# Cross-attention block on one core: first keys by token halves, residuals by quarters, sums of fc_w on GpSimd

## The chip, the cores and the metric

The kernel runs on 1 core of one Trainium2 chip. The metric is the device time of one execution in microseconds (us), the median over several runs. Engines are named as the profile names them: PE (TensorE, with its weight loads PEld), DVE (VectorE), ACT (ScalarE), POOL (GpSimd), SP (the engine from whose queue nearly all DMAs are issued).

## What is computed

One transformer block with cross-attention, in float32, for 8 batches of 256 tokens with 512 features, 16 heads of 32, and an MLP of 2048:

```python
def block(hidden_states, encoder_hidden_states, mask):
    x = layer_norm(hidden_states, ln1_w, ln1_b)
    q, k, v = x @ q_w + q_b, enc @ k_w + k_b, enc @ v_w + v_b      # 16 heads of 32
    attn = softmax(where(mask, q k^T / sqrt(32), -max))
    hidden = (attn v) @ cproj_w + cproj_b + hidden_states
    y = layer_norm(hidden, ln2_w, ln2_b)
    return hidden + gelu(y @ fc_w + fc_b) @ proj_w + proj_b
```

## The kernel before

**Tiling.** The batches are taken in 4 groups of 2 (512 tokens). All dense products are 2 by 2 block products by Strassen's scheme in 7 products: each operand has four quarters "11", "12", "21", "22" and three more slices for sums ("s2", "s3", "s4" of a weight, `A_SUMS`; "t1", "t2", "t4" of the tokens, `B_SUMS`), made by `sum_up` on an engine given by name. `strassen` returns seven closures p0 to p6, one for each product; a product of the projections is 4 matmuls of 256 columns in the code. The one exception is `eight`, which makes the first group's keys (`pkT`) as four plain quarter products k[0] to k[3], since these need no sums.

**Attention.** A group has 8 units (4 head groups by 2 batches). The loop over `units` issues for unit n, in this order: scores of unit n+2, softmax of n+2 (DVE L555, ACT L565), transposes of the probabilities of n (`turn_probs`, `ppt` L590, copied by DVE L593 and ACT L595), `divide` of n+1 on POOL (L579, four operations), and `attend` (`av`, L606). In between stand the lists `between[g, u, 0/1]`, which hold products of the next group's projections and transpositions (`turn_ctx` `pct`, `turn_x` `pxt`, `turn_hid` `pyt`), and `aside[g, u, 0..3]`, which hold loads, sums and the steps of the layer norms (`norm_over`: statistics, roots, `normalise` at L197). `begin` and `spread` put work there. Projected q, k and v go to DRAM and come back by head group (`load_qk`, `load_v`). `later` holds stores that are issued after `attend`.

**Output projection and residual.** `project_out(g)` gives `po`: products p0 to p6, u1 at L357 on DVE with the bias `cb`, the others at L362, L371 and L512; POOL L513 adds each quarter to the residual tile `resx`, one load of 1 MB for the group (`load_res`), whose quarter "12" first gets `cbd`, a difference of the bias halves (`bias_res`, POOL L506). Two stores write the sum to `hid_dram`. Group 3's projection follows the last unit, with the attention's last sums (`sum_att`, L626) on DVE.

**MLP.** It starts when the last projection is through, and runs group by group: four q, each with 7 products of fc (`pf`, L877; sums u and h on DVE at L932 to L949, gelu on ACT L920, sums of h on POOL L952 and L953), then 7 products of proj (`py`). In the first group, fc_w's quarters q+1 are summed on DVE (`sum_fc`, L167) while q runs; fcw[0] is summed on POOL in group 3's last units. fcw_3 takes the place of `cw` and is loaded after the attention; then follow on SP the four quarters `pw` of proj_w (1 MB each), `resm` (the hidden state for the residual, 1 MB, read back from `hid_dram`), and `hm` for the next group. POOL adds `projb` to all of `resm` at once (L959); DVE sums `pw` in four operations (L886).

**What sets the order.** The order is written out by hand: the program is recorded under a manual schedule, so each engine runs its instructions in the order of the code, and each DMA is issued from SP in the order of the code. A DMA has one of 8 semaphores and is issued when the eighth DMA before it is through. The 8 loads of the rows of biases and layer norm weights (`rows`) are issued from POOL; `turn_cols` turns them to columns (`cols`), which `made` of the keys needs.

The prologue ahead of the unit loop is, in its first part:

```python
        run(turn_ctx(0))
        load_ctx(1)
        ws["c"] = weight("cw", cproj_w)
        k, q, v, tx = project_qk(0, "kT"), project_qk(0, "qT"), project_v(0), turn_x(0)
        seen, roots, normalise = layer_norm(xs[0], "a0")
        run([k[0], *seen, roots, k[1], *normalise])
```

## Time and profile before

| What | Value |
|---|---|
| median of 3 runs | 761.43 us (761.0 to 761.65) |
| the profiled execution's own time | 761.83 us |
| its span in the profile | 759.6 us |
| granted PE clock, mean | 0.998 |
| busy: PE, DVE, ACT, POOL | 742.5, 367.9, 295.6, 379.1 us |
| data moved by DMA | 68.69 MB, 90 GB/s on the mean |
| MLP's first product starts, by the chain of waits | 361.79 us |
| one q of fc (7 products), one group of proj | 12.09 us, 48.36 us |

The span runs from the first to the last recorded instruction; the execution's own time is 2.2 us longer. A timeline line gives start, duration, engine, line of the code, operation, output and inputs, and in brackets the idle time ahead of it with the instruction that ended it. The waits list sums these idle times by the line that waited and the one waited for. A matmul of float32 is recorded as two instructions, so a Strassen product of the projections, 4 matmuls in the code, shows as x8.

### The profile page before, as it was taken

What the parts mean: (1) busy time and instruction counts of PE and PEld (TensorE: products, weight loads), DVE (VectorE), ACT (ScalarE), POOL (GpSimd) and SP (SyncE); (2) the same over time, 40 slices, a digit from 0 to 9 for tenths busy, and PEclk for the clock granted to TensorE, in tenths of its full rate; (3) what the DMA queues carried; (4) which work ended last, traced back from release to release, by engine and by line L of the source; (5) the groups of instructions that cost most, each with busy time, mean ns of one, the idle gap of its engine ahead of it and who ended that gap; (6) DMA issues with size and microseconds to landing.
All of it is one profiled execution on the core that took longest, in us unless ns stands there. A gap on an engine that the chain in (4) does not pass through costs nothing.

```text
span 759.6 us, 12080 instructions
## 1 busy us (share of the span) xinstructions
PE 742.5 (98%) x4441; PEld 624.1 (82%) x4441; DVE 367.9 (48%) x968; ACT 295.6 (39%) x857; POOL 379.1 (50%) x330
## 2 busy tenths in 40 slices
PE   7999999999999999898999999999999999999997
PEld 6988877887788777677888888888888888888886
DVE  3666755666466566657478442234412255122011
ACT  2267677766676777751332001230003300032200
POOL 3747599648664578996444520525305145032340
PEclk9999999999999999999999999999999999999999
DMA  9624522462234357423760004000040000200001
GB/s 297 220 70 129 168 85 81 130 211 70 98 106 150 98 182 246 145 70 111 228 215 2 1 0 167 1 0 1 1 144 22 2 1 0 77 36 0 1 1 56
DMA packets 55914, 68.69 MB, mean 90 GB/s; under 512 B 4740, under 2 KB 37552, under 8 KB 55728
## 3 DMA queue, kind: packets, MB, share of 16 engines
q1 hardware_dynamic: 55600, 67.91, 27.1%
q8 instruction: 35, 0.57, 0.3%
q14 instruction: 23, 0.19, 0.1%
q0 software_dynamic: 256, 0.02, 0.0%
HBM read 46.95 MB, written 20.97 MB: 89 GB/s over the span
## 4 chain that ended last, share of the span: by engine, by line
PE 91%; DVE 2%; ACT 2%; POOL 2%; DMA 1%; issue 1%; SPq 0%; DVEq 0%; POOLq 0%
PE pf L877 25%; PE py L877 25%; PE pqT L338 6%; PE ppt L590 6%; PE pv L338 5%; PE po L338 5%; PE av L606 5%; PE s L537 5%; PE pkT L338 4%; PE pkT L436 2%; ACT pr L565 1%; POOL x L197 1%; PE pct L210 1%; PE pyt L210 1%; PE pxt L210 1%
## 5 line engine op out<-in xcount | busy, mean ns | idle before, releaser
L877 PE MATMUL pf<-y,fcw 128*128 128x256 f32 x896 | 194.3, 379 | 0.8 <-DVE u L934 0.8
L877 PEld LDWEIGHTS pf<-y,fcw 128*128 128x128 f32 x896 | 170.2, 190 | 24.2 <-DVE u L934 1.2
L579 POOL TENSOR_TENSOR pr<-pr,rsum 128x512 f32<-128x512 f32 x128 | 129.4, 1042 | 74.9 <-DVE rsum L577 43.6
L565 ACT ACTIVATE pr<-pr,nmax 128x256 f32<-128x256 f32 x256 | 128.2, 503 | 60.5 <-DVE nmax L555 60.4
L555 DVE CUSTOM_DVE_ANT_0 pr<-s,mb 128x256 f32<-128x256 f32 x256 | 94.1, 413 | 46.2 <-PE s L537 33.2
L952 POOL TENSOR_TENSOR hs<-h,h 128x512 f32<-128x512 f32 x16 | 22.8, 1426 | 174.0 <-PE pf L877 127.5
L877 PE MATMUL py<-pw,h 128*128 128x256 f32 x384 | 84.9, 379 | 0.0
L877 PE MATMUL py<-pw_t,h 128*128 128x256 f32 x384 | 83.5, 379 | 0.0
L877 PEld LDWEIGHTS py<-pw_t,h 128*128 128x128 f32 x384 | 72.8, 190 | 9.7
L877 PEld LDWEIGHTS py<-pw,h 128*128 128x128 f32 x384 | 72.7, 190 | 9.7
L590 PEld LDWEIGHTS ppt<-ident,pr 128*128 128x128 f32 x512 | 57.3, 141 | 14.6 <-issue 9.0
L590 PE MATMUL ppt<-ident,pr 128*128 128x128 f32 x512 | 68.6, 276 | 0.2
L930 ACT COPY u<-pf 128x512 f32<-128x512 f32 x16 | 9.3, 584 | 150.0 <-PE pf L877 148.9
L920 ACT ACTIVATE h<-h,cols 128x256 f32<-128x256 f32 x96 | 43.4, 501 | 28.7 <-DVE h L949 14.2
L595 ACT COPY pt<-ppt 128x512 f32<-128x512 f32 x96 | 51.6, 571 | 4.9 <-PE ppt L590 4.9
L338 PE MATMUL pv<-vw,ctxT 128*128 128x256 f32 x224 | 52.4, 380 | 0.0
L920 ACT ACTIVATE h<-pf,cols 128x256 f32<-128x256 f32 x32 | 13.4, 470 | 98.1 <-PE pf L877 98.1
L338 PE MATMUL pqT<-xnT,qw 128*128 128x256 f32 x224 | 51.0, 379 | 0.0
L565 ACT ACTIVATION_READ_ACCUMULATOR pr<-pr,nmax 128x1 f32 x256 | 48.6, 190 | 0.0
L338 PEld LDWEIGHTS pv<-vw,ctxT 128*128 128x128 f32 x224 | 41.0, 190 | 5.4 <-ACT xnT L312 0.3
L338 PEld LDWEIGHTS pqT<-xnT,qw 128*128 128x128 f32 x224 | 41.3, 190 | 4.9
L606 PE MATMUL av<-pt,v 128*32 128x256 f32 x512 | 38.6, 386 | 2.9 <-ACT pt L595 2.1
(126 smaller groups left out, 970.0 us busy)
## 6 DMA issues: line engine op xcount, KB each, us to landing
ctx<-in_ctx_dram SPq DMA_DIRECT2D x16, 256.0 KB, 4.6
x<-in_x_dram SPq DMA_DIRECT2D x16, 256.0 KB, 5.4
v_dram<-st_v SPq DMA_DIRECT2D x16, 256.0 KB, 2.1
v<-v_dram SPq DMA_DIRECT2D x16, 256.0 KB, 3.9
resx<-in_x_dram SPq DMA_DIRECT2D x4, 1024.0 KB, 6.4
hid_dram<-resx SPq DMA_DIRECT2D x8, 512.0 KB, 2.8
hm<-hid_dram SPq DMA_DIRECT2D x16, 256.0 KB, 5.9
fcw<-in_L_xattn_fc_w_dram SPq DMA_DIRECT2D x16, 256.0 KB, 6.0
```

The lines of the kernel that those rows point to most:

```text
L210: nc.tensor.transpose(ps[:, ts(t, P)], xt[:, ts(c, P)], ident)
L338: nc.tensor.matmul(bank[n][:, i, :], l[:, c, ts(i, P)], r[:, c, :], start=first and i == 0 and c == 0, stop=last and c == HC - 1, skip_gro ...
L537: nc.tensor.matmul(banks[j][:, i, :], qT[j * HD : (j + 1) * HD, b * S + i * P : b * S + (i + 1) * P], kT[j * HD : (j + 1) * HD, b * SK : ( ...
L555: nc.vector.tensor_tensor_reduce(pr[:, j, i, :], banks[j][:, i, :], mbias[g][1][:, b, :], scale=-SCALE, scalar=FLT_MAX, op0=ALU.add, op1=A ...
L565: nc.scalar.activation(pr[:, j, i, :], pr[:, j, i, :], AF.Exp, bias=nmax[:, j, i : i + 1], scale=-1.0, accum_out=sums[:, j, i : i + 1],)
L579: nc.gpsimd.tensor_tensor(pr[:, j], pr[:, j], rsum[:, j, :, None].to_broadcast([P, NQ, SK]), ALU.mult,)
L590: nc.tensor.transpose(ps[:, kc, ts(i, P)], probs[n][:, j, i, ts(kc, P)], ident)
L595: nc.scalar.copy(pt, ps)
L606: nc.tensor.matmul(av[j * HD : (j + 1) * HD, :], vs[g, hg][:, b * NK + kc, ts(j, HD)], pts[n, j][:, kc, :], start=(kc == 0), stop=(kc == N ...
L877: nc.tensor.matmul(ps, lhsT, rhs, start=first, stop=last, skip_group_check=True)
L920: nc.scalar.activation(h[n][q][:, i, :], src[:, i, :], AF.Gelu_apprx_tanh, bias=col(c_fcb, half * HF + 2 * q + i), scale=1.0,)
L952: nc.gpsimd.tensor_tensor(h["s3"][q], h["11"][q], h["21"][q], ALU.subtract)
```

## The change

- **Start.** The first loads come in the order ctx_0, ctx_1, k_w's quarters 11 and 12, ctx_2, ctx_3, k_w's 21 and 22. Twelve transpositions of the constant `ident` into a PSUM tile that nobody reads are issued first. The first group's context is turned by token halves (`turn_first_ctx`), k[0] and k[1] stand behind one half each, and the sums of that context, formerly taken from PSUM on DVE, are made on POOL. pkT's last quarter is done in matmuls of 256 columns instead of 128.
- **Layer norms.** `norm_over` takes an engine; the statistics stand earlier and the normalise steps one or two to a slot. The one for `hm` goes from POOL to DVE.
- **Residuals.** `resx` becomes four tiles of a quarter each, loaded, biased, added and stored by the quarter. Group 0's are loaded at the end of unit 0 of group 1.
- **Group 3.** The slots of the 14 products and of the four `pyt` change; the sums of fcw[0] come earlier.
- **MLP.** The sums of fcw[1] to fcw[3] go from DVE to POOL; those of proj_w become 16 pieces on DVE; POOL adds the bias to two quarters of `resm` instead of all, and DVE adds it at u1 of `py` instead of ACT's copy. A_SUMS has another order of the same sums.

```diff
         a = Operand(wts.tile([P, 7, HC, S], F32, tag="w", bufs=4, name=name))
+        load_quarters(a, w, f, QUARTERS)
+        return a
+    def load_quarters(a, w, f, which):
...
             at = f + at * step
-            nc.sync.dma_start(a[n], src[:, k : k + HC, at : at + S])
-        return a
+            if n in which:
+                nc.sync.dma_start(a[n], src[:, k : k + HC, at : at + S])
...
         ("s3", "11", "21", ALU.subtract),
-        ("21", "21", "22", ALU.add),
-        ("s2", "21", "11", ALU.subtract),
+        ("s2", "22", "s3", ALU.subtract),
+        ("21", "s2", "11", ALU.add),
...
-    def load_tiles(pool, src, tag, name):
+    def load_tiles(pool, src, tag, name, between=None):
...
         for t in range(NT):
+            if between and t == NT // 2:
+                between()
...
                     nc.scalar.copy(chunk(x, c), halves(ps))
-                    sums = (second, x["t2"], x["t1"]), (first, x["t4"], x["t2"])
-                    if g:
-                        sums += ((second, x["12"], x["12"]),)
+                    sums = (
+                        (second, x["t2"], x["t1"]),
+                        (first, x["t4"], x["t2"]),
+                        (second, x["12"], x["12"]),
+                    )
...
             return [lambda c=c: piece(c) for c in (0, 2, 1, 3)]
+        def turn_first_ctx():
+            def piece(k):
+                if k == 0:
+                    ctxT[0] = tokens_operand(both, "cT", "ctxT_0")
+                for j in range(2):
+                    ps = turned(f"pct_0_{k}_{j}").rearrange("p (c s) -> p c s", c=HC)
+                    for t in range(2):
+                        for c in range(HC):
+                            nc.tensor.transpose(
+                                ps[:, c, ts(t, P)], ctxs[0][2 * k + t][:, ts(HC * j + c, P)], ident
+                            )
+                    to = ctxT[0][QUARTERS[2 * j + k]]
+                    if j == 0:
+                        nc.vector.tensor_copy(to, ps)
+                    else:
+                        nc.scalar.copy(to, ps)
+            return [lambda k=k: piece(k) for k in range(2)]
...
             if g == 0 and tag == "kT":
-                return [lambda n=n: eight(f"p{tag}_{g}", n, ws[w], src(), made) for n in QUARTERS]
+                return [lambda n=n: eight(f"p{tag}_{g}", n, ws[w], src, made) for n in QUARTERS]
...
             turns[0] ^= 1
-            step = P if n == "22" else S
...
                 for c in range(NC):
-                    for t in range(0, S, step):
-                        nc.tensor.matmul(
-                            bank[:, i, t : t + step],
-                            w[f"{n[0]}{c // HC + 1}"][:, c % HC, ts(i, P)],
-                            x[f"{c // HC + 1}{n[1]}"][:, c % HC, t : t + step],
-                            start=i == 0 and c == 0 and t == 0,
-                            stop=c == NC - 1,
-                            skip_group_check=True,
-                        )
+                    nc.tensor.matmul(
+                        bank[:, i, :],
+                        w[f"{n[0]}{c // HC + 1}"][:, c % HC, ts(i, P)],
+                        x()[f"{c // HC + 1}{n[1]}"][:, c % HC, :],
+                        start=i == 0 and c == 0,
+                        stop=c == NC - 1,
+                        skip_group_check=True,
+                    )
...
-        def load_res(g):
-            res[g] = residual(work, group_of(xf, g), "res", f"resx_{g}")
...
-        def quarter_of_res(g, n):
+        def quarter_of(src, n):
             o, k = int(n[0]) - 1, int(n[1]) - 1
-            return res[g][:, 2 * k : 2 * k + 2, ts(o, S)]
-        def bias_res(g):
-            r = quarter_of_res(g, "12")
-            nc.gpsimd.tensor_tensor(r, r, by_tiles(cbd), ALU.add)
+            return src[k * S : (k + 1) * S, ts(o, S)].rearrange("(t p) d -> p t d", p=P)
+        def load_res(g, *which):
+            for n in which:
+                r = work.tile([P, 2, S], F32, tag=f"res{n}", bufs=1, name=f"resx_{g}_{n}")
+                nc.sync.dma_start(r, quarter_of(group_of(xf, g), n))
+                res[g, n] = r
+                if n == "12":
+                    nc.gpsimd.tensor_tensor(r, r, by_tiles(cbd), ALU.add)
...
             def made(n, bank, u):
-                r = quarter_of_res(g, n)
+                r = res[g, n]
...
                 nc.gpsimd.tensor_tensor(r, r, st, ALU.add)
-                if n == "12":
-                    later.append(lambda: store_hid(g))
-            def store_hid(g):
-                for k in range(2):
-                    nc.sync.dma_start(
-                        hid_dram[g][k * S : (k + 1) * S, :].rearrange("(i p) d -> p i d", p=P),
-                        res[g][:, 2 * k : 2 * k + 2, :],
-                    )
+                later.append(lambda: nc.sync.dma_start(quarter_of(hid_dram[g], n), r))
...
-        def start_norm(g, tiles, tag):
-            norms[tag] = layer_norm(tiles[g], f"{tag}{g}", GP)
+        def start_norm(g, tiles, tag, eng):
+            norms[tag] = layer_norm(tiles[g], f"{tag}{g}", eng)
...
-        def norm_over(g, tiles, of_, tag, places):
-            begin(g, *places[0], start_norm, of_, tiles, tag)
+        def norm_over(g, tiles, of_, tag, places, eng=nc.gpsimd):
+            begin(g, *places[0], start_norm, of_, tiles, tag, eng)
...
                 norm_over(
-                    g, xs, g + 2, "a", [(2, 1), (2, 2), (3, 1), (3, 2), (3, 3), (4, 1), (4, 1), (4, 2), (4, 2)]
+                    g, xs, g + 2, "a", [(2, 1), (2, 1), (2, 2), (2, 2), (2, 2), (3, 1), (3, 2), (4, 1), (4, 2)]
...
         g = 1
-        begin(g, 1, 3, load_res, 0)
-        begin(g, 2, 2, bias_res, 0)
+        begin(g, 0, 3, load_res, 0, *QUARTERS)
...
         sums_at(att_in, 1, [(g, 6, 1), (g, 6, 2), (g, 7, 1), (g, 7, 2)])
-        begin(g, 5, 3, load_res, 1)
-        begin(g, 6, 2, bias_res, 1)
+        begin(g, 5, 3, load_res, 1, "11", "22", "21")
+        begin(g, 6, 3, load_res, 1, "12")
...
             project_out(1) + project_out(2),
-            [(u, i, 1) for u in range(8) for i in range(2) if (u, i) not in ((3, 1), (7, 1))],
+            [(u, i, 1) for u in range(8) for i in range(2) if (u, i) not in ((6, 1), (7, 1))],
         )
-        begin(g, 3, 3, load_res, 2)
-        begin(g, 4, 2, bias_res, 2)
-        begin(g, 7, 3, load_res, 3)
-        begin(g, 7, 3, bias_res, 3)
+        for u, h, which in (
+            (2, 2, ("11",)), (3, 2, ("22", "21")), (4, 2, ("12",)), (5, 3, ("11",)), (7, 3, ("22", "21"))
+        ):
+            begin(g, u, 3, load_res, h, *which)
...
         norm_over(
-            g, hids, 0, "m", [(1, 1), (1, 2), (2, 1), (2, 2), (2, 3), (3, 1), (3, 2), (4, 1), (4, 2)]
+            g, hids, 0, "m", [(1, 1), (1, 2), (2, 1), (2, 2), (2, 2), (3, 1), (3, 2), (4, 1), (4, 2)], V
...
-        for c, (u, i) in enumerate(((5, 1), (6, 1), (7, 1), (7, 1))):
+        for c, (u, i) in enumerate(((6, 1), (6, 1), (7, 1), (7, 1))):
...
             fcw[q] = weight(f"fcw_{q}", fc_w, q * S)
-        def sum_fc(q, *which):
-            sum_up(V, fcw[q], A_SUMS, *which)
...
             g,
-            [(5, 2), (6, 2), (6, 3), (7, 2)],
+            [(2, 2), (2, 3), (4, 2), (5, 2)],
...
-        load_ctx(0)
-        ws["k"] = weight("kw", k_w)
+        warm = ps_t.tile([P, G], F32, tag="pt", name="warm")
+        for t in range(12):
+            nc.tensor.transpose(warm[:, ts(t % NT, P)], ident, ident)
+        ws["k"] = Operand(wts.tile([P, 7, HC, S], F32, tag="w", bufs=4, name="kw"))
+        ctxs[0] = load_tiles(
+            work, group_of(ef, 0), "ctx", "ctx_0", lambda: load_quarters(ws["k"], k_w, 0, ("11", "12"))
+        )
+        load_quarters(ws["k"], k_w, 0, ("21", "22"))
...
-        run(turn_ctx(0))
+        first = turn_first_ctx()
+        k, q, v, tx = project_qk(0, "kT"), project_qk(0, "qT"), project_v(0), turn_x(0)
+        seen, roots, normalise = layer_norm(xs[0], "a0")
+        run([first[0], k[0], first[1], k[1]])
...
         ws["c"] = weight("cw", cproj_w)
-        k, q, v, tx = project_qk(0, "kT"), project_qk(0, "qT"), project_v(0), turn_x(0)
-        seen, roots, normalise = layer_norm(xs[0], "a0")
-        run([k[0], *seen, roots, k[1], *normalise])
+        run([*seen, roots, k[2], *normalise])
...
         make_mask(0)
-        run([k[2], *tx])
+        run([*tx, k[3]])
...
         sum_up(V, xnT[0], B_SUMS, 0, 1)
-        run(k[3:])
...
         sum_up(GP, ws["v"], A_SUMS, *ALL)
-        nc.gpsimd.tensor_tensor(cbd, cb[:, :S], cb[:, S:], ALU.subtract)
+        sum_up(GP, ctxT[0], B_SUMS, 0, 1)
         run(q[:1])
-        sum_up(GP, ctxT[0], B_SUMS, 2)
...
         run([roots, q[5]])
+        sum_up(GP, ctxT[0], B_SUMS, 2, 3)
+        nc.gpsimd.tensor_tensor(cbd, cb[:, :S], cb[:, S:], ALU.subtract)
...
         o = project_out(3)
+        load_res(3, "12")
...
             )
-        def sum_pw(i):
-            to, a, b = (("t1", "12", "11"), ("t2", "22", "t1"), ("12", "22", "12"), ("t4", "21", "t2"))[i]
-            nc.vector.tensor_tensor(pw[to], pw[a], pw[b], ALU.subtract)
+        def sum_pw():
+            for to, a, b, op in (
+                ("12", "22", "12", ALU.subtract),
+                ("t2", "12", "11", ALU.add),
+                ("t1", "22", "t2", ALU.subtract),
+                ("t4", "21", "t2", ALU.subtract),
+            ):
+                for p in range(0, HF, 2):
+                    c = slice(p, p + 2)
+                    nc.vector.tensor_tensor(pw[to][:, c], pw[a][:, c], pw[b][:, c], op)
+                    yield
+        pw_sums = sum_pw()
+        pbd = wpool.tile([P, HD2], F32, name="pbd")
+        nc.gpsimd.tensor_tensor(pbd, projb[:, :HD2], projb[:, HD2:], ALU.subtract)
...
+            def out_quarter(b, k):
+                return ht[:, 2 * b : 2 * b + 2, ts(k, HD2)]
+            def by_tiles(row):
+                return row[:, None, :].to_broadcast([P, 2, HD2])
...
                 ahead = g == 0 and q + 1 < HF // 2
+                def some_pw(n):
+                    if g == 0 and q:
+                        for _ in range(n):
+                            next(pw_sums)
...
                 if ahead:
-                    sum_fc(q + 1, 0, 1)
+                    sum_up(nc.gpsimd, fcw[q + 1], A_SUMS, 0, 1)
+                some_pw(1)
...
                 if ahead:
-                    sum_fc(q + 1, 2, 3)
+                    sum_up(nc.gpsimd, fcw[q + 1], A_SUMS, 2, 3)
+                some_pw(2)
...
                 nc.vector.tensor_tensor(h["21"][q], bank[5], u2, ALU.add)
+                some_pw(1)
...
                 nc.gpsimd.tensor_tensor(h["21"][q], h["21"][q], h["22"][q], ALU.add)
-                if g == 0:
-                    for i in ((), (0,), (1, 2), (3,))[q]:
-                        sum_pw(i)
...
                     ht = residual(work, hid_dram[g], "resm", f"resm_{g}")
-                    nc.gpsimd.tensor_tensor(
-                        ht, ht, projb[:, None, :].to_broadcast([P, NT, D]), ALU.add
-                    )
+                    for b, bias in ((0, projb[:, :HD2]), (1, pbd)):
+                        o = out_quarter(b, 0)
+                        nc.gpsimd.tensor_tensor(o, o, by_tiles(bias), ALU.add)
...
             }
-            def out_quarter(b, k):
-                return ht[:, 2 * b : 2 * b + 2, ts(k, HD2)]
...
             proj(bank[1], "11", "11", True, False)
-            nc.scalar.copy(u1, bank[1])
+            nc.vector.tensor_tensor(u1, bank[1], by_tiles(projb[:, HD2:]), ALU.add)
+            if g == 0:
+                for _ in pw_sums:
+                    pass
```

## The prediction

> **What bounds the kernel now.** I read the busy line and the shares of the chain first, then the waits of TensorE (PE), then timelines around each place that the diff touches.
>
> ```profile
> PE 742.5 (98%) x4441; PEld 624.1 (82%) x4441; DVE 367.9 (48%) x968; ACT 295.6 (39%) x857; POOL 379.1 (50%) x330
> ...
> PE 91%; DVE 2%; ACT 2%; POOL 2%; DMA 1%; issue 1%; SPq 0%; DVEq 0%; POOLq 0%
> ```
>
> PE holds 91% of the chain. The number of products stays the same, so the change can win only PE's waits, and lose by new ones. They are few (us in total, times, longest):
>
> ```profile
> PE pct L210 <- DMA ctx<-in_ctx_dram: 5.1, 4, 3.5
> PE av L606 <- ACT pt L595: 2.1, 2, 1.9
> PE po L338 <- DVE po_u L357: 1.8, 1, 1.8
> PE pxt L210 <- POOL x L197: 1.6, 2, 1.1
> PE pf L877 <- DVE u L934: 0.8, 1, 0.8
> ```
>
> Next the timeline at these places (start, duration, engine, line):
>
> ```profile
> 6.48 3.03 PE L210 MATMUL pct<-ident,ctx 128*128 128x128 f32 x13 [0.17 <-DMA ctx<-in_ctx_dram]
> 100.11 8.40 POOL L197 TENSOR_SCALAR x<-x,mv_a,rstd_a 128x512 f32<-128x512 f32 x4
> 108.56 0.77 PE L210 MATMUL pxt<-ident,x 128*128 128x128 f32 x5 [1.12 <-POOL x L197]
> 316.87 1.53 PE L606 MATMUL av<-pt,v 128*32 128x256 f32 x16 [1.91 <-ACT pt L595]
> 349.33 1.49 DVE L626 TENSOR_TENSOR att<-att 128x256 f32<-128x256 f32 x1
> 352.88 3.73 PE L338 MATMUL po<-cw,att 128*128 128x256 f32 x16 [1.82 <-DVE po_u L357]
> 375.82 1.27 POOL L952 TENSOR_TENSOR hs<-h,h 128x512 f32<-128x512 f32 x1 [9.45 <-ACT h L920]
> 377.75 4.29 SPq L226 DMA_DIRECT2D resm<-hid_dram  x1
> 390.78 4.53 POOL L959 TENSOR_TENSOR resm<-resm,projb 128x2048 f32<-128x2048 f32 x1 [12.34 <-DMA resm<-hid_dram]
> 393.52 4.02 DVE L167 TENSOR_TENSOR fcw<-fcw 128x512 f32<-128x512 f32 x2
> 407.48 3.72 PE L877 MATMUL pf<-y,fcw 128*128 128x256 f32 x16 [0.79 <-DVE u L934]
> ```
>
> The reader should see that POOL waits idle for `resm` until 390.78 and nobody minds, because the `fcw` sums run on DVE. Below, T0 = 361.79 is where the MLP's first product starts; from there PE is packed but for the 0.79.
>
> [...] the 13 transposes above take 0.233 each, the later ones 0.109. No later PE wait exceeds 1.91[...]. [...] L952 at 395.28 starts as the waiting L959 ends. [...] two fcw sums on DVE take 4.02 beside L959's 4.53, but 1.41 at 381.43; an L626 sum takes 1.43 to 1.49 on DVE beside POOL's fcw sums.
>
> **Part by part** (PE time, negative is faster).
>
> 1. *First keys by halves.* Half of ctx and k's quarters 11, 12 are loaded first. The four ctx tiles now land at about 3.4, 4.2, 5.7, 6.4, so k's two quarters take the third and fourth place and the last is here by 6.5 to 7[...]. Eight transposes and a copy (.4 to .6) put k[0] at about 6.2 to 6.5 and, at 16 × .216 = 3.46, its end near 9.8. But `turn_cols` stands behind k[0], and `rows` is whole only at 11.05 (last issue on POOL's queue 5.35, 5.7 to landing). PE waits about 1.3, then turns the other half (8 × .109) and waits for its copy: k[1] at 12.85 instead of 13.36. To q: 2 × 3.455 + 1.75 + 3.455 = 12.12, against 12.42 before (pkT_22 in half-width matmuls costs .12 more, the rest is small gaps). q starts at 24.97 for 25.78: **−0.8** (0 to −2). Moving four ctxT sums to POOL and cbd behind them is covered by PE's seven q products (12.1).
> 2. *Statistics earlier, one normalise per slot.* Four L197 in a row (8.40) hold PE at 108.56 and 187.91. Start to start the stalled transposes take 2.21 and 1.58, unstalled .87: 1.34 + .71 = **−2.05** (−1.5 to −2.1). At the places of the new order POOL has slots between its divides (4 × 1.01 of a period near 8 to 11).
> 3. *Residuals by quarters, group 1.* The four loads of group 0's residual are now issued at the end of unit 0 and the bias add on quarter 12 is put at once on POOL, ahead of the next divide (L579, at 142.43 before). On SP they stand behind x (issued 139.94), mask and v_1, which is issued at 142.84 and lands 5.1 later, at 147.94. Two 256 KB quarters more make 149.5 for quarter 12; add 1.27, then divides at 1.01: pr0 at 151.8, pr1 at 152.9. PE's ppt of that unit started at 150.74 and needs them: **+1.65** (0.5 to 2.8). Behind that add wait only the four divides, for which ppt waits. The same pattern in the other groups has its load issued where the queue is short: 0. The 12 more loads and 8 more stores put about 20 × .45 = 9 us on SP, over 280 us and among loads made a unit or more ahead: 0 (up to +0.5). Stores now wait on L513 in SP's FIFO, with the next kT, qT and v loads behind them, a unit ahead of need: 0.
> 4. *Group 3.* A product now fills slot (3,1), where the 1.91 wait stood: the period stays at 8.08. Its place (6,1) is freed of 1.73, and one transposition (4 × .13) goes from (5,1) to (6,1), where unit 5's 8.33 falls to 8.08: −1.73 − .25 + .45 = −1.5, near −1.6 with the shorter `av`. The fcw[0] sums leave the last slots for (2,2) to (5,2); then DVE's three L626 (1.43 + 1.49 + 1.48) run at about .45 each and po_u is ready before PE asks. From the end of the last `av`'s pieces to T0 it is 15.29, where 1.0 + 7 × 1.727 = 13.1 is needed: −2.2. Against it the hm normalise comes to DVE (4 × .48, in softmax slots) and two loads wait on POOL: +.5. **−3.3** (−2 to −4.2).
> 5. *MLP.* The fcw sums move from DVE to POOL, the projection sums become 16 pieces of .69 on DVE, the residual's bias add becomes 2 × 1.27 on POOL and another row on DVE. The 0.79 at 407.48 came from L886's 2.28 + 3.35 ahead of u: **−0.8**. But POOL's order becomes hs and h of q=0, both `resm` adds (they wait for the load), then fcw[2]'s sums. [...] PE's second product of q=2 needs s3 and s2 at T0 + 24.17 + 1.73 = T0 + 25.9 (two q of 12.09). Before, resm landed at T0 + 28.9; no one noticed. In the changed kernel the last hid store is one quarter, so fcw_3 is issued from about T0 + 2.65 (before T0 + 5.02), its last quarter lands between T0 + 7.4 and T0 + 10.0 (before T0 + 12.4), and the chain of pw and resm loads adds 16.5: T0 + 23.9 to 26.5, I take 25.1. Then 2 × 1.27 (adds), 2 × 1.27 (s3, s2), .15 to be seen: T0 + 30.3. **+4.4** (2.4 to 6.0; nothing excludes less if the queue drains sooner, hence rival A). Behind POOL's wait are s4, `21` and hs of q=1; PE needs the first two in the same q, later, the rest at T0 + 48.
>
> Sum: −0.8 − 2.05 + 1.65 − 3.3 − 0.8 + 4.4 = −0.9. The profiled execution took 761.83 (span 759.6 and 2.2 around it): 760.9. It stands 0.4 above the median of 761.43, so 760.5.
>
> **Rivals.** *A, the resm wait is hidden.* If resm lands before T0 + 20.7 (25.9 less 5.2 of POOL work), the +4.4 falls away: 756.1. For: SP's queue is ahead of before and quarters are smaller. Against: 1 MB of fcw_3, 4 MB of pw and 1 MB of resm are moved in order, and they took 24 from the first issue before. *B, slower: the clock drops.* [...] a matmul that takes .216 takes .43[...]: 760.5 + 2.6 = 763.1, and 764.7 if the wait is 6.0. [...] PE may keep its clock. *C, the group-1 divide is on time* (quarter 12 landed before 148.4, as the v_1 load is not what limits it): −1.65, 758.9. *D, the start doesn't do what it says*, since rows bind k[0]'s end rather than the context: 0 instead of −0.8, 761.3.
>
> **How the numbers follow.** About 0.2% (1.5 us) is what a measurement of this kernel can tell from no change. Forecast with D: .45, between 759 and 762.5; C .12; A .18; B .25. A and most of C are faster, B is mostly slower, and the forecast's middle lies 0.9 below before, so a third of it passes the lower bound: faster .40, same .36, slower .24. The likeliest is 760.5. Leaving out a tenth at either end, in A's lower and B's upper half, gives 756.0 to 764.3.
>
> **What would show it.** In the changed profile: PE waits for POOL L167 `fcw` once near T0 + 26 for about 4.4, with `resm` adds before it; no `pxt` waits; a ppt wait on POOL L579 near 150 of about 1.65; no po_u wait; pkT_11 near 6.4 and a wait at ps_cols; the granted clock at 9 in the slice of the fcw wait, or lower if B is right. A resm landing before T0 + 20.7, or a PE wait of several us at another place, would make it wrong.

## The result and the profile after

The changed kernel took 767.63 us on the median of 6 runs (764.47 to 769.32), the kernel before 762.53 on the same chip. The ratio is 1.0066, with a 95% interval of 1.0039 to 1.0092: slower by 0.4 to 0.9%. The prediction said 760.5, 0.9 less than before, with a range of 756.0 to 764.3. The profiled execution took 769.02 (span 767.2), 7.2 more than the profiled one of before.

I read the profile in the same order as before. The busy line and the shares of the chain:

```profile
PE 749.7 (98%) x4437; PEld 628.9 (82%) x4437; DVE 360.5 (47%) x970; ACT 293.0 (38%) x851; POOL 378.3 (49%) x346
...
PE 84%; POOL 6%; issue 3%; DMA 2%; ACT 2%; DVE 1%; SPq 1%; POOLq 0%; DVEq 0%
```

PE is busy for 7.2 us more. The twelve transpositions of the constant account for 2.8 of that; the products are otherwise nearly the same, so some of them ran slower. And POOL's share of the chain has grown from 2% to 6%. The waits of PE (us in total, times, longest):

```profile
PE pf L903 <- POOL fcw L171: 5.7, 1, 5.7
PE ppt L610 <- POOL pr L599: 3.3, 5, 2.0
PE warm L796 <- POOL neg_half L110: 1.4, 1, 1.4
PE ps_cols L476 <- DMA rows<-in_L_xattn_fc_b_dram: 1.1, 1, 1.1
PE av L626 <- ACT pt L615: 0.4, 2, 0.2
PE pkT L462 <- DVE ctxT L324: 0.3, 1, 0.3
```

The waits on L210, po_u and u are gone as forecast, the forecast waits on fcw and pr are there, both longer than forecast. To find where time was won and lost I set the starts of `av` (one for each unit) beside each other, from the timelines of both kernels:

| Landmark | before | after | shift |
|---|---|---|---|
| group 0, unit 0 | 63.69 | 62.84 | -0.85 |
| group 0, unit 5 | 110.99 | 108.95 | -2.04 |
| group 0, unit 6 | 119.29 | 118.41 | -0.88 |
| group 1, unit 1 | 148.53 | 147.66 | -0.87 |
| group 1, unit 2 | 159.55 | 162.97 | +3.42 |
| group 1, unit 5 | 192.06 | 194.77 | +2.71 |
| group 3, unit 5 | 333.28 | 335.75 | +2.47 |
| group 3, unit 6 | 340.54 | 342.29 | +1.75 |
| group 3, unit 7 | 346.34 | 348.75 | +2.41 |
| MLP's first product | 361.79 | 362.10 | +0.31 |
| first product of `py` | 411.03 | 418.92 | +7.89 |

Between the landmarks the periods (from one `av` to the next) agree, but for 0.15 in group 0's unit 3. So two places lose much: 4.29 at unit 2 of group 1, and 7.58 in the MLP's first fc. A third, group 0's unit 6, gives back 1.16 of 1.34 just won, and group 3's unit 7 loses 0.66. The timeline of the MLP's place, SP, POOL and PE:

```profile
375.65 2.92 SPq L232 DMA_DIRECT2D resm<-hid_dram  x1
...
388.65 1.26 POOL L1014 TENSOR_TENSOR resm<-resm,projb 128x512 f32<-128x512 f32 x1 [10.09 <-DMA resm<-hid_dram]
389.87 1.26 POOL L1014 TENSOR_TENSOR resm<-resm,pbd 128x512 f32<-128x512 f32 x1
391.08 5.17 POOL L171 TENSOR_TENSOR fcw<-fcw 128x512 f32<-128x512 f32 x4
...
393.74 25.34 PE L903 MATMUL pf<-y,fcw 128*128 128x256 f32 x104 [5.74 <-POOL fcw L171]
```

The chain is the one that the prediction wrote: resm lands, two adds, two of fcw[2]'s four sums, then PE. But the 13 products behind it take 25.18 to 418.92, where 13 x 1.727 is 22.45. The view by stretches shows why (stretch, sum, PE, PEld, DVE, ACT, POOL; then the granted clock, DMA share and GB/s):

```profile
385.00:390.00 5.00, 3.00 (x14) 2.29 (x13) 2.67 (x5) 2.40 (x5) 1.35 (x2) 1.00 0.77 282
390.00:395.00 5.00, 1.26 (x3) 1.08 (x4) 0.00 (x0) 0.00 (x0) 4.84 (x5) 0.73 0.01 3
395.00:400.00 5.00, 5.00 (x15) 4.00 (x15) 0.69 (x1) 0.00 (x0) 4.92 (x5) 0.59 0.00 0
400.00:405.00 5.00, 5.00 (x25) 4.41 (x24) 2.13 (x3) 1.42 (x4) 4.26 (x4) 1.00 0.00 0
```

The clock falls in the wait, to 0.73 and 0.59 on the mean of a stretch, and in 395 to 400 PE passes 15 instructions where it passes 25 at 1.00, from 400 on. Unit 2 of group 1 has the same in small:

```profile
149.60 1.27 POOL L534 TENSOR_TENSOR resx<-resx,cbd 128x512 f32<-128x512 f32 x1 [9.64 <-DMA resx<-in_x_dram]
150.82 8.03 POOL L599 TENSOR_TENSOR pr<-pr,rsum 128x512 f32<-128x512 f32 x8
...
151.92 0.66 PE L610 MATMUL ppt<-ident,pr 128*128 128x128 f32 x4 [1.98 <-POOL pr L599]
152.91 0.76 PE L610 MATMUL ppt<-ident,pr 128*128 128x128 f32 x4 [0.34 <-POOL pr L599]
153.47 3.51 PE L367 MATMUL pqT<-xnT,qw 128*128 128x256 f32 x8
```

POOL's add waited 9.64 for its load, with the divides behind it; PE waited 1.98 and 0.34; then eight pqT instructions took 3.51, where they take 1.89 elsewhere. The granted clock was 0.50 from 153.4 to 156.7:

```profile
153.40:156.70 3.30, 3.30 (x10) 2.65 (x9) 0.65 (x5) 1.57 (x5) 3.30 (x4) 0.50 0.95 352
156.80:157.80 1.00, 1.00 (x6) 0.88 (x5) 0.78 (x2) 0.00 (x0) 1.00 (x3) 1.00 0.06 23
```

Of the 4.29 lost here, about 2.67 is waiting and 1.62 the clock.

### The profile page after: what moved, and what is told of

Its sections match the earlier page's. It is cut to its first block, busy times and chain, and to the rows that moved or that the text cites. A ratio compares the mean times of both kernels' runs of the same rounds, so it can differ in the third digit from the quotient of the medians.

```text
span 767.2 us, 12111 instructions
## 1 busy us (share of the span) xinstructions
PE 749.7 (98%) x4437; PEld 628.9 (82%) x4437; DVE 360.5 (47%) x970; ACT 293.0 (38%) x851; POOL 378.3 (49%) x346
## 4 chain that ended last, share of the span: by engine, by line
PE 84%; POOL 6%; issue 3%; DMA 2%; ACT 2%; DVE 1%; SPq 1%; POOLq 0%; DVEq 0%
PE py L903 25%; PE pf L903 23%; PE ppt L610 5%; PE pqT L367 5%; PE pkT L367 5%; PE pv L367 5%; PE po L367 5%; PE s L557 4%; PE av L626 4%; POOL pr L599 3%; DMA resm<-hid_dram 2%; PE pkT L462 1%; ACT pr L585 1%; PE pxt L216 1%; PE pyt L216 1%
## 5 line engine op out<-in xcount | busy, mean ns | idle before, releaser
L903 PE MATMUL pf<-y,fcw 128*128 128x256 f32 x896 | 196.9, 383 | 5.7 <-POOL fcw L171 5.7
L903 PEld LDWEIGHTS pf<-y,fcw 128*128 128x128 f32 x896 | 172.0, 192 | 30.0 <-POOL fcw L171 6.1
L1007 POOL TENSOR_TENSOR hs<-h,h 128x512 f32<-128x512 f32 x16 | 20.3, 1270 | 181.2 <-PE pf L903 139.0
L367 PE MATMUL pqT<-xnT,qw 128*128 128x256 f32 x224 | 52.6, 388 | 0.0
```

Of the source, the lines that this page charges most:

```text
L367: nc.tensor.matmul(bank[n][:, i, :], l[:, c, ts(i, P)], r[:, c, :], start=first and i == 0 and c == 0, stop=last and c == HC - 1, skip_gro ...
L903: nc.tensor.matmul(ps, lhsT, rhs, start=first, stop=last, skip_group_check=True)
L1007: nc.gpsimd.tensor_tensor(h["s3"][q], h["11"][q], h["21"][q], ALU.subtract)
```

## The experiments

Each kernel is the changed one (or the one before, where said) with one edit. The times are medians, the ratio is to runs of the kernel before on the same chip.

**1. The bias adds on resm behind fcw's sums** (`e1_bias_after_sums`).

```diff
                 if q == 0:
                     ht = residual(work, hid_dram[g], "resm", f"resm_{g}")
-                    for b, bias in ((0, projb[:, :HD2]), (1, pbd)):
-                        o = out_quarter(b, 0)
-                        nc.gpsimd.tensor_tensor(o, o, by_tiles(bias), ALU.add)
                     if g + 1 < NG:
                         load_hid(g + 1)
+                if q == 2:
+                    for b, bias in ((0, projb[:, :HD2]), (1, pbd)):
+                        o = out_quarter(b, 0)
+                        nc.gpsimd.tensor_tensor(o, o, by_tiles(bias), ALU.add)
```

> The changed kernel, with the two bias adds on the residual tile resm put behind the sums of fcw[3] (end of q=2) instead of ahead of those of fcw[2]. Theory (POOL in order: the resm landing holds the fcw[2] sums, and the wait of 5.74 then drops PE's clock for about 2.65 more): no PE wait on fcw in the MLP, the clock stays full there, time near 767.6 - 7.5 = 760 (from 758.5 to 761.5), first group's fc back to about 48.4 from 57. Rival (the fcw[2] sums are late by themselves, because POOL is slower at them or because fcw_2 or y is late): a wait of 2 us or more stays, 764 or more. Rival (the clock drop has another cause than the wait): a drop to about 0.6 near 395 stays and costs 2.6: 762.

758.58, ratio 0.9952 (0.9936 to 0.9967). No wait on fcw is left, and PE keeps its clock of 1.00 through 385 to 405. So two adds of 1.26, whose result is first read at 440.71 in the changed kernel, made it slower than before: by their place in POOL's queue, not by their length. The gain is 9.1 where 7.5 was expected. Between the two profiles the first fc is 8.6 shorter. The divide of group 1, which this edit does not touch, made PE wait 1.02 instead of 1.98, with the clock at 1.00 from 150 to 160, and that unit is 2.6 shorter.

**2. The bias add of group 1 in its old slot** (`e2_bias_at_slot`).

```diff
+        def bias_res(g):
+            nc.gpsimd.tensor_tensor(res[g, "12"], res[g, "12"], by_tiles(cbd), ALU.add)
...
-                if n == "12":
-                    nc.gpsimd.tensor_tensor(r, r, by_tiles(cbd), ALU.add)
+                if n == "12" and g:
+                    bias_res(g)
...
         begin(g, 0, 3, load_res, 0, *QUARTERS)
+        begin(g, 2, 2, bias_res, 0)
```

> The changed kernel, with group 0's four residual loads where they are, but the bias add of quarter 12 put at unit 2 of group 1 (where the kernel before had it) instead of at once behind its load. Theory (the add waits for its load at the head of POOL's queue and holds the divide of unit 2; PE waits 2.7 us for it and loses 1.6 more by a dropped clock): unit 1's period in group 1 goes from 15.3 back to 11.0, time near 767.6 - 4 = 763.6 where the clock had dropped, 765 where it had not. Rival (the loads themselves delay what the unit needs, kT, qT or v of the next head group): the period stays above 13 us, 766 to 768.

764.27, ratio 1.0023 (1.0015 to 1.003), 3.4 less than the changed kernel. The shift of `av` against the changed kernel's profile is -0.05 up to unit 1 of group 1 and -4.34 from unit 2 on: the unit's whole loss. The loads alone cost nothing.

**3. Both** (`e3_both`): the two diffs above together.

> The changed kernel with both moves of the two runs before it. Theory: the two costs are independent, at 232 us from each other: 767.6 - 7.5 - 4.2 = 756 (755 to 757.5), faster than the kernel before by about 6, and the runs lie closer together (within 1 us)[...]. Rival (the costs are in series with something else that comes next, such as the wait of DVE for pw, or of the next unit's operands): 758 to 762.

756.85, ratio 0.9924 (0.9907 to 0.9941); its runs lie within 0.31 us. In its profile unit 1 of group 1 has its old period of 11.02 again and the first fc takes 48.35, so each edit takes away the loss of its own place. The gains of the medians don't add up (9.1 and 3.4 alone, 10.8 together), since what the clock costs differs from run to run: the mean clock is 0.993 to 0.998 in the runs of experiment 2, 0.997 to 0.999 in those of experiment 1 and 0.999 or 1.0 in these. Without the two places the change is faster than before by 0.6 to 0.9%.

**4. Filling the wait** (`e4_filler`): 48 transposes of the constant ahead of the waiting product.

```diff
+                if g == 0 and q == 2:
+                    for _ in range(4):
+                        fill = ps_m.tile([P, G], F32, tag="mm", name=f"fill_{_}")
+                        for t in range(12):
+                            nc.tensor.transpose(fill[:, ts(t % NT, P)], ident, ident)
                 fc(bank[6], "s2", "t2", q, True, True)
```

> The changed kernel, with 48 transposes of the constant (48 x 0.109 = 5.2 us, into a PSUM tile that nobody reads) put on PE just ahead of the product that waits for fcw[2]. Theory (the wait itself is unchanged, but PE is not idle in it, so the clock holds): the product starts at the same time after the MLP's start (T0 + 31.6), the clock near 395 stays full, time near 767.6 - 2.6 = 765 (764 to 766). Rival (the slow matmuls behind the wait are not from idle PE but from what runs beside them): the clock figure or the slow stretch stays, 767 to 768. Should resm land sooner than the 26.5 us after T0 of the profiled run, the filler costs up to 1 us.

765.64, ratio 1.0043 (1.003 to 1.0056): 2.0 less than the changed kernel. PE's timeline:

```profile
385.20 5.40 PE L987 MATMUL fill<-ident 128*128 128x128 f32 x48
391.05 21.20 PE L903 MATMUL pf<-y,fcw 128*128 128x256 f32 x97 [0.44 <-POOL fcw L171]
```

and by stretches:

```profile
390.00:395.00 5.00, 4.56 (x24) 3.88 (x23) 0.89 (x2) 0.00 (x0) 4.84 (x5) 1.00 0.00 0
395.00:400.00 5.00, 5.00 (x24) 4.38 (x24) 1.89 (x4) 1.63 (x4) 4.84 (x4) 1.00 0.00 0
```

The product starts 31.75 after the MLP's first, as it did (31.80), but the clock stays at 1.00 and 24 instructions pass in 5 us instead of 15. The 13 products behind the wait take 22.55 for 25.18. The slow products behind the wait come from PE's idleness, not from POOL, whose sums run beside them here too (4.84 in each stretch).

**5. fcw's sums back on DVE** (`e8_fcw_on_dve`).

```diff
-                    sum_up(nc.gpsimd, fcw[q + 1], A_SUMS, 0, 1)
+                    sum_up(nc.vector, fcw[q + 1], A_SUMS, 0, 1)
```

The same is done for sums 2 and 3.

> One part of the change undone: the sums of fcw[1] to fcw[3] go back to DVE, all else as changed. Theory (the move to POOL is what exposes PE to the resm load): no fcw wait, clock full in the MLP, 767.6 - 7.5 = 760 or less, the same as with the bias adds moved (758.6), since the 0.79 wait of before came from the undivided proj_w sums. Rival (DVE becomes late with 4 fcw sums and 4 pieces in each q, or holds for pw's landing): waits on u or h of 0.5 to 2 us in q=1 to q=3, 760.5 to 763.

760.43, ratio 0.9966 (0.9954 to 0.9978). No wait on fcw, u or h appears. With a clock of 0.999 one run took 758.69, like experiment 1; the others have 0.996 to 0.997, and in the profile the clock falls behind the divide of group 1, outside this edit (0.82, 0.50 and 0.83 in the stretches of 2 us from 152 to 158). The first fc takes 48.35 in the profile, as in experiments 1 and 3. So the move of fc_w's sums to POOL brought nothing that the pieces of proj_w's sums did not bring already, and it opened PE to the wait for resm.

**6. resm ahead of pw** (`e11_resm_first`).

```diff
+        ht = residual(work, hid_dram[0], "resm", "resm_0")
         for n, f, d in (("11", 0, 0), ("12", 0, HD2), ("22", HF, HD2), ("21", HF, 0)):
...
+                    if g:
                         ht = residual(work, hid_dram[g], "resm", f"resm_{g}")
```

> The changed kernel with group 0's resm loaded ahead of the four pw quarters of 1 MB instead of behind them; POOL's order is untouched. Theory (POOL waits for the landing, and resm lands at T0 + 26 only since 4 MB of pw go before it): resm lands before T0 + 14, POOL's adds are done before fcw[2]'s sums are asked for, no wait on fcw, time 758.5 to 760.5, like the run with the adds moved. The pw quarters land some 3 us later: DVE's first piece (q=1, T0 + 19.7) then waits for pw_22 to about T0 + 24, which stops the sums of u and h behind it and could cost PE 1 to 3 us (rival: 760.5 to 763). Rival (POOL's order, not the landing, holds the sums): the wait on fcw stays at 4 or more, 767.

759.07 (758.24 to 762.98), ratio 0.9963 (0.9946 to 0.9979). POOL's adds run at 379.88, right behind h, without a wait, and PE has no wait in the MLP. The feared hold of DVE for pw costs PE nothing. The landing behind 4 MB of pw is what POOL waited for. Group 1's divide is as the change has it; in the profiled run (761.71) PE waited 2.0 for it, and the run's mean clock was 0.996, for 0.999 in the fastest (758.24).

**7. A ladder of gaps** (`e5_gap_ladder`), on experiment 3, in the MLP of groups 1 to 3: POOL makes a tile z by one to four adds and PE turns it.

```diff
+                if g:
+                    nc.gpsimd.tensor_tensor(z, h["22"][q], h["22"][q], ALU.subtract)
+                    for _ in range(full - 1):
+                        nc.gpsimd.tensor_tensor(z, z, z, ALU.add)
+                    for _ in range(half):
+                        nc.gpsimd.tensor_tensor(z[:, 0], z[:, 0], z[:, 0], ALU.add)
                 fc(bank[1], "12", "21", q, False, True)
+                if g:
+                    nc.tensor.transpose(fill[:, :P], z[:, 0, :P], ident)
```

> Measures the clock's answer to one idle gap of PE by itself. The kernel with both bias adds moved, and in groups 1 to 3 of the MLP, where PE is else packed, each q gets one transpose of a tile that POOL makes by a chain started at the fourth product: 1 to 4 adds of 1.27 and one half add of 0.73, so that PE should idle about 1.2, 1.7, 2.4, 3.0 (group 1), 1.7, 2.4, 3.0, 3.7 (group 2), 1.7, 2.4, 3.7, 4.3 us (group 3). Theory[...]: no drop at 1.2, some but not all at 1.7 to 3.0, all at 3.7 and 4.3; a drop costs 1.3 to 1.9 us each[...]. Rival[...]: drops at 3.7 and 4.3 alone. Time: 756.9 + 31 of gaps + 5 to 12 of drops, 793 to 800.

794.0, from two runs; what follows is read from one profile. The gaps came out as 0.86, 1.29, 1.98, 2.41, 3.10 and 3.52 us. Three of the stretches, each from 0.5 ahead of the gap to 7.5 behind its end; the first two are gaps of 1.98, the third one of 3.10:

```profile
491.57:501.55 9.98, 8.00 (x31) 6.39 (x30) 1.38 (x2) 3.65 (x9) 2.55 (x4) 0.83 0.00 0
586.29:596.27 9.98, 8.00 (x38) 6.74 (x37) 1.54 (x3) 4.03 (x9) 4.16 (x5) 1.00 0.00 0
617.19:628.29 11.10, 8.00 (x31) 6.43 (x30) 2.65 (x5) 3.44 (x8) 3.59 (x5) 0.85 0.00 0
```

| Gap, us | 0.86 | 1.29 | 1.98 | 2.41 | 3.10 | 3.52 |
|---|---|---|---|---|---|---|
| places | 1 | 3 | 3 | 2 | 2 | 1 |
| with a fall of the clock | 0 | 0 | 1 | 1 | 2 | 1 |

The same gap drops the clock at one place and not at another: of the gaps of 1.98, that at 492.06 and not those at 586.78 and 698.7; of the two of 2.41, one. A fall takes 7 of 38 instructions from the stretch, some 1.5 us (7 x 0.216); the granted clock gives 1.7 (0.17 of 9.98). The rival, drops at the two longest steps alone (3.10 and 3.52 as they came out), is wrong. By slices of 1 us the first gap of 1.98 looks so:

```profile
492.05:493.05 1.00, 0.01 (x1) 0.00 (x0) 0.00 (x0) 0.95 (x3) 0.92 (x2) 1.00 0.00 0
493.05:494.05 1.00, 0.00 (x1) 0.01 (x2) 0.00 (x0) 0.68 (x2) 0.86 (x2) 1.00 0.00 0
494.05:495.05 1.00, 1.00 (x5) 0.92 (x6) 0.00 (x0) 0.00 (x0) 0.00 (x0) 0.93 0.00 0
495.05:496.05 1.00, 1.00 (x3) 0.77 (x3) 0.00 (x0) 0.00 (x0) 0.00 (x0) 0.50 0.00 0
496.05:497.05 1.00, 1.00 (x4) 0.76 (x3) 0.00 (x0) 0.00 (x0) 0.00 (x0) 0.50 0.00 0
497.05:498.05 1.00, 1.00 (x4) 0.81 (x3) 0.69 (x1) 0.13 (x1) 0.00 (x0) 0.50 0.00 0
498.05:499.05 1.00, 1.00 (x5) 0.83 (x5) 0.00 (x0) 0.77 (x2) 0.00 (x0) 0.86 0.00 0
```

and the second, behind which PE passes 6 where it passes 3 or 4 above:

```profile
586.77:587.77 1.00, 0.01 (x1) 0.00 (x0) 0.00 (x0) 0.95 (x3) 0.92 (x2) 1.00 0.00 0
587.77:588.77 1.00, 0.00 (x1) 0.01 (x2) 0.00 (x0) 0.68 (x2) 0.86 (x2) 1.00 0.00 0
588.77:589.77 1.00, 1.00 (x5) 0.92 (x6) 0.00 (x0) 0.00 (x0) 0.00 (x0) 1.00 0.00 0
589.77:590.77 1.00, 1.00 (x6) 0.87 (x6) 0.00 (x0) 0.00 (x0) 0.00 (x0) 1.00 0.00 0
```

Nor does the length of one gap alone decide it: a gap of 2.41 (508.15) left the clock at 1.00, while in experiment 9's profile waits of 1.24 and 0.35 in the start were followed by 0.76 on the mean of 10 to 15 and 0.90 of 15 to 20. What sets such places apart was not shown.

**8. The layer norm's places alone**, on the kernel before (`e9_norm_places_only`).

```diff
                 norm_over(
-                    g, xs, g + 2, "a", [(2, 1), (2, 2), (3, 1), (3, 2), (3, 3), (4, 1), (4, 1), (4, 2), (4, 2)]
+                    g, xs, g + 2, "a", [(2, 1), (2, 1), (2, 2), (2, 2), (2, 2), (3, 1), (3, 2), (4, 1), (4, 2)]
```

> The kernel before, with the new places of the first layer norm's steps alone. Theory: -1.34 at 108.6 of which about 1.16 is given back by the next scores (their PSUM bank is freed by ACT), and -0.71 at 187.9 that stays: -0.9 in all, 761.7 on a run of before at 762.6. Rival (the prediction's step: both waits are gone for good): -2.05. Rival (POOL's divides are put late by the normalise steps in their new slots): 0 or more.

761.4, ratio 0.9987 (0.998 to 0.9995), 1.07 less. The period of group 0's unit 4 falls from 9.65 to 8.31, that of unit 5 rises from 8.30 to 9.46. In this profile the clock also fell behind the old 1.91 wait of `av` near 317 (0.50 from 318 to 320, where the profile of before has 1.00): the same wait at the same place costs 1.6 in one profile and nothing in another.

**9. The pxt copies on DVE** (`e6_xnT_on_dve`), on experiment 3. What gives the 1.34 back is seen in the changed kernel's timeline:

```profile
109.64 1.43 ACT L341 ACTIVATE xnT<-pxt,cols 128x512 f32<-128x512 f32 x2
109.95 2.30 PE L557 MATMUL s<-kT,qT 32*128 32x256 f32 x16
```

The scores take 2.30 for the usual 1.15. They use the PSUM banks in which `turned` puts pxt, and ACT copies pxt out only at 109.64 to 111.07, since it comes to it behind its exponentials. DVE is idle there from 108.5 to 112.

```diff
-                if g == 0 and c % 2:
+                if (g == 0 and c % 2) or (g == 2 and c < 2):
                     nc.vector.tensor_scalar(
```

> The kernel with both bias adds moved, and the copies of the first two pxt of group 0's unit 5 (L341, group 2's tokens) on DVE instead of ACT. Theory (the 1.34 won by earlier normalise steps at 107 was given back in the next scores, s taking 2.30 for 1.15, since pxt sits in a PSUM bank of the scores and ACT copies it out only at 109.64 behind its exponentials, while DVE is idle from 108.5): unit 6's period falls from 9.46 to 8.3, time 756.85 - 1.1 = 755.7. Rival (the scores wait for the load of kT and qT): period stays 9.46, no change.

755.67, ratio 0.9913 (0.9901 to 0.9926), 1.2 less than experiment 3; the period goes from 9.46 to 8.38. The cause is shown.

**10. The start alone**, on the kernel before (`e10_start_only`), with the start's part of the diff:

```diff
-        load_ctx(0)
-        ws["k"] = weight("kw", k_w)
+        warm = ps_t.tile([P, G], F32, tag="pt", name="warm")
...
-        run(turn_ctx(0))
+        first = turn_first_ctx()
...
+        run([first[0], k[0], first[1], k[1]])
...
+        sum_up(GP, ctxT[0], B_SUMS, 0, 1)
```

> The kernel before with the new start alone (loads by halves, constant turned ahead, first keys by token halves, the context's sums on POOL). Theory of the prediction: -0.8, 761.7 on a run of before at 762.5, less in runs where rows lands late. Theory after the runs (the wait for rows of 0.6 to 2.1 takes back half of it, and in a part of the runs drops the clock for 1.7 more): between -0.8 and +1, median -0.1 to -0.6, wide scatter. Rival (the start brings its full gain of 2 or more): 760.5.

761.91, ratio 0.999 (0.9979 to 1.0002): 0.9 less; the interval includes no change. In its profile rows was late (a wait of 1.94), and behind that wait k[1] and k[2] took 8.28 for 7.17; the run's mean clock was 0.994.

**11. More covered** (`e7_all_covered`): experiment 9, `turn_cols` behind k[1], and in group 3 the bias add and one sum of fcw[0] behind the divides.

```diff
+            if n == "12":
+                turn_cols()
+                held.pop()()
             if n == "11":
-                turn_cols()
-            made(n, bank, None)
+                held.append(lambda: made(n, bank, None))
+            else:
+                made(n, bank, None)
...
+                if n == "12" and g not in (0, 2):
+                    bias_res(g)
...
+        begin(g, 5, 2, bias_res, 2)
-            [(2, 2), (2, 3), (4, 2), (5, 2)],
+            [(2, 2), (2, 3), (4, 2), (6, 2)],
```

> A version meant to beat both kernels: both bias adds moved, the pxt copies on DVE, and two more moves. turn_cols stands behind k[1] instead of k[0] (its wait for rows, 0.6 to 2.1 in the runs, is then covered by the other half's turning and k[1]); in group 3 the bias add of group 2's quarter 12 goes to unit 5 and one sum of fcw[0] to unit 6, both behind the divide that they held. Theory: -1.2 to -2 at the start and no dropped clock there (which cost 1.7 in the profiled run with the pxt copies on DVE), -0.9 in units 6 and 7 of group 3: 755.7 - 2.3 = 753.4 (752.8 to 754.5). Rival (the next wait takes over at the start: q's product waits for xnT or its weights; or the later fcw sum is late for the MLP): 754.5 to 756.

756.29, ratio 0.9913 (0.9897 to 0.993): no gain. The wait for rows was gone, but k[2] waited 1.17 for ACT to clear k[0]'s bank, pxt 0.64 for x, and pxt took 3.01 for 1.91, at a clock of 1.00: its first four instructions came 0.46 apart, behind the four normalise steps on DVE. The start lost 1.9 against experiment 3. In group 3 units 6 and 7 won 1.0. Here the wait was moved, not removed.

**12. The same with `turn_cols` in its place** (`e12_best`): the last diff without its first part.

> The version before (e7_all_covered) with turn_cols back behind k[0], where the change has it. The run with it moved lost 1.9 at the start (k[2] waited for the delayed kT, pxt for x) and won 1.0 in group 3. Theory: the start's loss goes, the gains of the pxt copies (1.07) and of group 3 (1.0) stay: 756.3 - 1.9 = 754.4 where the start keeps its clock, 756 where the wait for rows drops it; below e6_xnT_on_dve (755.67) by 1.0 at like clocks. Rival (the loss at the start was the rows landing late in that run, not the move): 755.5 to 756.5.

754.5, ratio 0.9911 (0.9892 to 0.993), the lowest time of all. Its ratio does not part it from experiments 9 and 11 (both 0.9913), since the kernel before took 761.42 beside it, for 762.47 and 762.81 beside those. In the profile, units 6 and 7 of group 3 are 1.0 shorter than in experiment 3. Four runs at a clock of 0.999 or 1.0 took 754.0 to 754.6, two at 0.996 and 0.997 took 756.3 and 756.5. What is left of PE's waits:

```profile
PE warm L800 <- POOL neg_half L110: 1.4, 1, 1.4
PE ps_cols L476 <- DMA rows<-in_L_xattn_fc_b_dram: 1.3, 1, 1.3
PE pkT L462 <- DVE ctxT L324: 0.7, 2, 0.3
PE av L628 <- ACT pt L617: 0.4, 2, 0.2
```

## Why the prediction was wrong

**Step 1, the start: right in this profile, in part by luck.** -0.8 forecast, -0.85 in the profile, with the forecast wait for rows (1.3 forecast, 1.06 measured; 0.6 to 2.1 in the runs that show it). But in the eleven profiles with this start the first `av` begins from 1.07 earlier to 0.88 later than in the profile of before, and experiment 10 does not part the gain from none. That the clock could fall behind this wait (1.24 in experiment 9's profile, and 0.76 over 10 to 15) was not seen.

**Step 2, the layer norms: wrong by 1.15.** Of -2.05, the 0.71 stayed and 1.16 of the 1.34 went back at the next scores. The step asked what ends the wait of pxt, not who waits for pxt to be copied out of the shared banks (experiments 8 and 9).

**Step 3, the residual of group 1: the wait right, the fall of the clock behind it left out.** Quarter 12's add started at 149.60 for 149.5 forecast. But steps 1 and 2 had by then moved PE 0.87 ahead. The loads were issued earlier by as much, yet v_1 took 6.1 us to land instead of 5.1, and that makes the wait 2.67 instead of 1.65. In the profiles of experiments 1 and 4, which leave this place as it is, v_1 took 5.1 and 5.0 and the unit lost 1.66 and 1.51, as forecast. The fall of the clock, which the step put at nothing, adds 1.62; experiment 2 takes both away.

**Step 4, group 3: -2.4 instead of -3.3.** The slots gave -0.25 and -0.72, the end of the attention -2.10. Unit 7 lost 0.66 instead: step 3 had put the loads of the other groups at nothing ("issued where the queue is short: 0"), but group 2's quarter 12 landed only at 334.78 and kept its add waiting on POOL to 334.90, and that add and the fcw[0] sum held the next divides (experiments 11 and 12).

**Step 5, the MLP: the mechanism right, the wait in its range, the fall of the clock left to a rival.** The 0.79 is gone. fcw_3's last quarter landed at T0 + 10.15 where the range ended at 10.0, and resm's adds started at T0 + 26.55, where 25.1 was taken from a bound of 23.9 to 26.5; that makes 5.74 for 4.4. In experiment 2's profile, with this place unchanged, resm landed at T0 + 25.2 and the wait was 4.63. Rival B, the fall of the clock behind this wait, cost 2.7; the 2.6 put on it was the author's estimate, which no trace had shown, and it was held for the less likely case. The pace is near the .43 a matmul that it named: 12 instructions pass in 394 to 399, at a clock of 0.50, for 25 in 400 to 405, at 1.00.

Together: -0.9 + 1.15 + 2.64 + 0.9 + 1.3 + 2.7 = 7.8. The landmarks give 7.89 up to `py`; the profiled executions differ by 7.2. More than half of it, 1.62 + 2.7 = 4.3, is the two falls of the clock, which the sum had put at nothing. This is the step that failed most. That such waits leave the clock alone was the author's estimate and not shown: behind the start, no wait of PE in the profile of before was longer than 1.91, and behind that one the clock stayed at 1.00. The prediction priced no fall behind a wait of 1.65, and only as a rival behind one of 4.4. This profile has falls behind 1.98 (with 0.34 after it) and behind 5.74, and the ladder behind gaps from 1.98 on. Without the two falls this profile would still be some 3.5 slower than before, for the terms of steps 2 and 4 and the later landings of this run.

That the median moved by 5.1 rather than 7.2 fits this too: whether a wait drops the clock differs from run to run. The three runs of the changed kernel with a mean clock of 0.993, the profiled one among them, took 768.4 to 769.3, the one with 0.998 took 764.5. The kernel before has waits of 1.91 and 1.82, at 317 and 353, of which the first was followed by a fall in experiment 8's profile, and its own runs spread from 759.8 to 764.5.

## What to carry to other kernels

An instruction that waits for a load should not stand in an engine's queue ahead of work that a bound engine will ask for, even if it is short and its load is expected early: two adds of 1.26 cost 9.1 here. When a wait is removed, ask next who waits for the freed result's buffer, and take every due time in the frame that the other edits have already moved. A wait of 2 us on TensorE may cost 3.6 (1.98 and 1.62 here): cover it by other products, or at least by transposes of a constant (48 in 5.40 us held the clock at 1.00 in experiment 4), where it can't be removed.

## What the runs showed of the hardware

In the changed kernel's profile TensorE's granted clock was 0.50 from 153.4 to 156.7, behind waits of 1.98 and 0.34, which cost 1.62, and from 392.3 to 399.0, in and behind the wait of 5.74, which cost 2.7. In experiment 2's it was 0.67 and 0.65 on the mean of 385 to 390 and 390 to 395, around a wait of 4.63. In the ladder, with PE else packed, it fell at none of four gaps of 0.86 and 1.29, at one of three of 1.98, at one of two of 2.41, and at all three of 3.10 and 3.52. A wait of 1.91 at the same place left it at 1.00 in the profile of before and was followed by 0.50 in experiment 8's. What decides between places and runs was not shown. 48 transposes that nobody needs, 5.40 us of PE, kept it at 1.00 from 385 to 400, where the wait without them had 0.73 and 0.59 from 390 on (experiment 4).
